# Attention with one shared key head: the order of loads and small steps at the front of the kernel, and the place of token loads and one mask conversion after it

## The chip, the cores and the metric

The kernel runs on one core of a Trainium2 chip. The metric is device time in microseconds (us) of one execution, lower is better. The core has five engines with an instruction queue each: TensorE (PE, matrix products and transposes), VectorE (DVE), ScalarE (ACT), GpSimd (POOL) and SyncE (SP), which here issues nearly all transfers. Each engine takes its instructions strictly in the order in which the program writes them and waits at an instruction until its operands and its buffers are ready; engines wait for each other through semaphores.

## The reference

64 batches of 128 tokens with 512 features. Each is normalised, projected to 16 query heads of 64, and to one key and one value head that all query heads share; a null key and value (from `cond`) stand ahead of the 128 keys. Scores get a bias per head, a mask per batch and a causal mask; the softmax goes over 129 keys. The output projection is normalised again and added to the input.

```python
xn = layernorm(x, g_in)
q = (xn @ Wq).reshape(b, n, H, DH).transpose(0, 2, 1, 3) * scale
kv = xn @ Wkv
k, v = (kv[..., :DH], kv[..., DH:])
k = jnp.concatenate([nk, k], axis=1)      # null key ahead
v = jnp.concatenate([nv, v], axis=1)      # null value ahead
sim = jnp.einsum('bhid,bjd->bhij', q, k) + bias
sim = jnp.where(causal_mask, neg, sim)
sim = jnp.where(mask_p[:, None, None, :], sim, neg)
attn = jax.nn.softmax(sim, axis=-1)
out = jnp.einsum('bhij,bjd->bhid', attn, v)
out = out.transpose(0, 2, 1, 3).reshape(b, n, INNER) @ Wo
x = x + layernorm(out, g_out)
```

All is in float32. The null key and value are subtracted from keys and values, and the null bias from the bias, so that the null column itself is zero before the softmax.

## The kernel before

Four batches make a group, 16 groups in all. For batch `m`, `load_x` brings its tokens (from group 2 on, a mixed quarter of a group's tokens under the same numbering); `norm_stats` (DVE, one small power on POOL), `norm_nmr` (DVE) and `norm_apply` (DVE for group 0, ACT after it) normalise them in place; `norm_T` transposes them on PE with a copy by ACT for groups 0 and 1, `tokens_T` with `tokens_out` and `tokens_in` (DVE and two transfers over DRAM) from group 2 on. `kv_mm` and `kv_out` make keys and values, `keys_T` and `values_spread` bring them into the layout of the products through DRAM. Queries of group 0 come from `q_half(c, h)`, eight chunks `c` for two halves `h` of the group; those of later groups from seven products in place of eight (`product`, with sums of weights and tokens made by `weight_sum` on DVE and `token_sum` on POOL).

Order is written out by hand: instructions go to each engine as the lines of the program stand. It has three parts.

The front (lines 1138 to 1222): group 0 is loaded, normalised and projected, `w_q` and `w_kv` are scaled by the gain (`weights_q`, `weights_kv`), the bias is made causal on POOL (`causal(u)`, u is the half of the heads) and the null bias is taken from it on DVE (`null_shift(u)`), group 1 is normalised. `load_second` issues the loads behind the weights: first half of the bias, null bias, null key and value, second half of the bias, mask of group 0, the null value once more as a column (`nv2`), tokens of batches 4 to 7, mask of group 1. On SP nothing overtakes: a load whose buffer isn't free, or which the queue holds back, holds all behind it. Tokens live in three buffers (`xp`), only batches 3 and 4 in two others; so batch 7 takes the buffer of batch 2 and its load waits for `norm_T(2)`.

The steps (`step_a` for even n, `step_b` for odd n, from n = -2): step n makes a quarter of the queries of a later group and a quarter of its keys and values, the exponentials of batch n+1, and, in `region`, scores of batch n+2 and values of batch n; output products run in pairs of batches. At the end of `step_a` the tokens n+12 and n+13 are loaded, behind the stores of that step. At the end of each fourth `step_b` (f == 3), `mask_neg(g)` turns the mask of the next group into numbers (`mneg`, line 485, DVE); `bias_add` on POOL adds it to the bias, and `scores_add` on DVE (line 528) adds the scores from PSUM.

The last steps (`last_step`) hold no projection and are not touched.

PSUM for scores has one buffer (`ps_s`): the second half of a batch's scores is written only when `scores_add` has read the first. `kv_mm` and `norm_T` share two buffers (`ps_w`).

Of the kernel before, what the change touches and what calls it, by code (L numbers as in the profile page):

```python
# [17 lines left out]
def kernel(  # L18
# [60 lines left out]
    B, N, DIM = x.shape  # L79
# [6 lines left out]
    GB = 4  # L86
    NG = B // GB
# [12 lines left out]
    XB = 3  # L100
# [13 lines left out]
    def load_x(m):  # L114
        g, t = divmod(m, GB)
        pool, tag = (rp, "res") if m in (XB, XB + 1) else (xp, "x")
        xs[m] = pool.tile([P, DIM], FP, tag=tag, name=f"x_{m}")
        if g < 2:
            nc.sync.dma_start(out=xs[m], in_=x[m])
        else:  # L120
            nc.sync.dma_start(
                out=xs[m], in_=x[g * GB : (g + 1) * GB, t * Q : (t + 1) * Q, :]
            )
# [13 lines left out]
    def load_mask(g):  # L137
        m8s[g] = gp.tile([P, TOK], U8, tag="m8", name=f"m8_{g}")
        nc.sync.dma_start(
            out=m8s[g],  # L140
            in_=mask[g * GB : (g + 1) * GB].rearrange("b n -> (b n)").partition_broadcast(P),
        )
# [23 lines left out]
    nc.sync.dma_start(out=wkv, in_=w_kv.rearrange("(kc p) f -> p kc f", p=P))  # L166

    def load_second():
        load_bias(1)
        nc.sync.dma_start(out=nbh, in_=null_bias.partition_broadcast(P))  # L170
        nc.sync.dma_start(
            out=nkv, in_=cond[0:2].rearrange("r d -> (r d)").partition_broadcast(P)
        )
        load_bias(0)
        load_mask(0)
        for r in range(2):
            nc.sync.dma_start(
                out=nv2[r * DH : (r + 1) * DH, :], in_=cond[1].unsqueeze(1)
            )
        for m in range(XB + 1, 2 * GB):  # L180
            load_x(m)
        load_mask(1)

    def load_bias(u):
        rows = slice(u * DH, (u + 1) * DH)
        bias_r = attn_bias.rearrange("(u f r) i j -> u r i f j", u=2, r=2)[u]
        for r in range(2):
            rf = slice(r * NF, (r + 1) * NF)
            nc.sync.dma_start(out=biasp[rows, rf, LK], in_=bias_r[r, 0:DH, :, 0:NL])
            nc.sync.dma_start(out=biasp[rows, rf, UK], in_=bias_r[r, DH:N])  # L190
# [77 lines left out]
    def norm_apply(m):  # L268
        if m >= GB and m not in xnmr:
            norm_nmr(m)  # L270
        mv, rstd = stats.pop(m)
        xm = xs[m]
        if m < GB:
            nc.vector.tensor_scalar(
                xm, xm, mv[:, 0:1], rstd, ALU.subtract, ALU.mult
            )
        else:
            nc.scalar.activation(  # L278
                xm, xm, AF.Identity, bias=xnmr.pop(m), scale=rstd
            )  # L280
# [188 lines left out]
    def q_out(g, c, toks, tag, name=None):  # L469
        lo = toks.start // N  # L470
        o = q_part(g, c, lo, lo + 2)
        p = prod[tag].rearrange("p (t h i) -> p t h i", t=2, h=2)
        if name is None:
            nc.scalar.copy(o, p)  # L474
        else:
            k = kept.pop(name).rearrange("p (t h i) -> p t h i", t=2, h=2)
            nc.vector.tensor_tensor(o, p, k, ALU.add)  # L477
# [302 lines left out]


    def weights_q(kc):
        if kc in (2, 0):
            nc.vector.tensor_scalar(
                wq[:, kc, :], wq[:, kc, :], gin8[:, kc : kc + 1], None, ALU.mult
            )
        else:
            nc.scalar.activation(
                wq[:, kc, :], wq[:, kc, :], AF.Copy, scale=gin8[:, kc : kc + 1]
            )  # L790
# [32 lines left out]
    def step_a(n):  # L823

        g, f = divmod(n + 6, GB)
        q = g < NG
        p12, p4 = n - 1, n - 3
        first, third = paired(p12), paired(p4)
        e, nb = n + 1, n + 2
        soft = 0 < n  # L830
        if q and f == 0 and g + 1 < NG:
            load_mask(g + 1)
        if third:
            out_product(p4, 4, ps_y, "X", start=False)
        if soft:
            exps(e, 0, 0, 3)
        if third:
            pair_stats(p4)
        if n == 2:
            token_sum(g, 3)  # L840
            token_sum(g, 4)
        if 0 < n:
            bias_add(nb)
        if third:
            pair_pow(p4)
            out_part(p4 + 1, 0, "X")
        max_hi()
        kv_late = not first
        if n == 0:
            norm_stats(10)  # L850
            exps(1, 1, 0, 4)
        if q:
            if not kv_late:
                kv_out(n + 6, kv_mm(n + 6))
            if f == 0:
                q_tile(g)
            product(g, f, 1, ps_q, "a")
        if soft:
            exps(e, 0, 3, 6)
        if q:  # L860
            keep("a", "p1")
            product(g, f, 2, ps_w, "w")
            q_out(g, f, lo_t, "w", "p1")
        if soft:
            exps(e, 0, 6)
            rinv(e, 0)
        if q:
            if f == 0 and n > 2:
                token_sum(g, 3)
            product(g, f, 6, ps_q, "a", start=False)  # L870
            keep("a", "u2")
        if n == 0:
            exps(1, 1, 4)
            rinv(1, 1)
            scale(1, 1)
        if soft:
            scale(e, 0)
        if third:
            pair_stats(p4 + 1)
            pair_pow(p4 + 1)  # L880
            pair_nmr(p4)
        if soft:
            exps(e, 1, 0, 2)
        if third:
            pair_norm(p4)
            pair_gain(p4)
            pair_residual(p4)
            store(p4)
        if q:
            if f == 0 and n > 2:  # L890
                token_sum(g, 4)
            product(g, f, 5, ps_q, "c")
        if first:
            out_product(p12, 1, ps_y, "X")
        if soft:
            exps(e, 1, 2, 3)
        if first:
            out_keep("X", "yp1", "yp1")
        if third:
            pair_nmr(p4 + 1)  # L900
        if q:
            product(g, f, 7, ps_q, "a", start=False)
            keep("a", "u3")
            q_out(g, HC + f, hi_t, "c", "u3")
            if kv_late:
                kv_out(n + 6, kv_mm(n + 6))
        if third:
            pair_norm(p4 + 1)
        if first:
            out_product(p12, 2, ps_w, "w")  # L910
        if third:
            pair_gain(p4 + 1)
        if first:
            out_part(p12, 0, "w", "yp1")
        if third:
            pair_residual(p4 + 1)
            store(p4 + 1)
        if q:
            product(g, f, 3, ps_q, "c", start=False)
            q_out(g, f, hi_t, "c", "u2")  # L920
        if soft:
            exps(e, 1, 3)
            rinv(e, 1)
            scale(e, 1)
        if n == 2:
            residual(0)
            store(0)
        if n == -2:
            scores(1, 0)
            scores_add(1, 0)  # L930
            scores_max(1, 0)
            blocks_T(0)
        if n == 0:
            norm_apply(10)
            norm_stats(11)
            tokens_T(10)
            load_x(13)
        if q:
            product(g, f, 4, ps_q, "a", start=False)
            q_out(g, HC + f, lo_t, "a")  # L940
        if n == 0:
            norm_apply(11)
        if n == -2:
            scores(1, 1)
            scores_add(1, 1)
            late_max.append(1)
        for m in (n + 12, n + 13):
            if m < B and n:
                load_x(m)

    def step_b(n):

# [52 lines left out]
        if q:  # L1005
            product(g, f, 7, ps_q, "a", start=False)
            keep("a", "u3")
            q_out(g, HC + f, hi_t, "c", "u3")
            if kv_late:
                kv_out(n + 6, keys_values())  # L1010
            if n == 1:
                out_mm(0)
# [29 lines left out]
        if q:  # L1042
            product(g, f, 4, ps_q, "a", start=False)
            q_out(g, HC + f, lo_t, "a")
            if f == 3:
                keys_T(g)
                values_spread(g)
                if g < NG:
                    mask_neg(g)
        if second:  # L1050
            out_product(p, 3, ps_y, "Y", start=False)
# [102 lines left out]
    norm_stats(3)  # L1154
    q_half(0, 0)
    norm_apply(2)
    norm_T(2)
    q_half(1, 0)
    norm_apply(3)
    norm_T(3)  # L1160
    weights_kv()
    norm_stats(4)
    norm_apply(4)
    q_half(2, 0)
    causal(1)
    norm_stats(5)
    norm_apply(5)
    null_shift(1)
    q_half(3, 0)
    norm_T(4)  # L1170
    for m in range(GB):
        kv_out(m, kv_mm(m))
    norm_stats(6)
    norm_stats(7)
    norm_nmr(6)
# [18 lines left out]
    weight_sum(4)  # L1194
    for c in range(4):
        q_half(c, 1)
    load_late()
    load_x(8)
    load_x(9)
# [75 lines left out]
```

## Time and profile before

| | |
|---|---|
| median of 3 runs | 1103.41 us (1102.82 to 1104.4) |
| the profiled execution's own time | 1104.52 us |
| its span in the profile | 1102.7 us |
| granted TensorE clock, mean | 0.993 |
| PE busy / DVE / ACT / POOL | 1077.4 / 800.9 / 694.9 / 702.1 us |
| from HBM / to HBM | 67.45 MB / 35.65 MB |
| front: PE starts the first scores | 47.88 us |

All times inside the profile are microseconds from the start of the span. PE is TensorE's matmul row, PEld its weight loads, SPq the transfers that SP issues. A row of the timeline has start, duration, engine, line, operation, output and inputs, shapes and count, and in brackets how long the engine had been idle before it and what ended that. Rows merge neighbouring instructions; durations of matmuls overlap a little, so the step from one start to the next is the better measure. The granted clock is given as a share of full speed.

### The profile page before, as it was taken

How to read it: one execution, taken by the hardware profiler on the slowest of the kernel's cores; microseconds unless marked ns; L12 is line 12 of the kernel's file. 1: busy time of each engine (PE TensorE's matmuls, PEld its weight loads, DVE VectorE, ACT ScalarE, POOL GpSimd, SP SyncE). 2: the span in 40 equal slices, each digit the busy share in tenths (PEclk: the TensorE clock that was granted, in tenths of full speed). 3: DMA queues.
4: the chain of work that ended last, by engine and by line, in shares of the span. 5: the costliest groups of instructions: out<-in, count | busy, mean ns of one | idle time of the engine just before them, and what ended most of it. 6: DMA issues, size and time to landing. Idle time of an engine off the chain costs nothing.

```text
span 1102.7 us, 29987 instructions
## 1 busy us (share of the span) xinstructions
PE 1077.4 (98%) x11780; PEld 900.2 (82%) x11780; DVE 800.9 (73%) x1545; ACT 694.9 (63%) x2779; POOL 702.1 (64%) x517
## 2 busy tenths in 40 slices
PE   7999999999999999999999999999999999999997
PEld 6876788888888888888888888888888888888653
DVE  4667578786787878678687787878678787657772
ACT  3355566666766666666666676666676666567682
POOL 2465757676675766757586675767667576665572
PEclk9999999999999999999999999999999999999999
DMA  7414242333334242333324234233333424111211
GB/s 198 139 44 120 77 117 76 112 90 111 82 100 122 70 120 78 118 97 92 105 80 133 69 90 133 70 118 89 112 84 99 121 67 125 58 59 41 68 60 67
DMA packets 67980, 105.03 MB, mean 95 GB/s; under 512 B 8448, under 2 KB 32640, under 8 KB 66048
## 3 DMA queue, kind: packets, MB, share of 16 engines
q1 hardware_dynamic: 67024, 102.07, 31.1%
q8 instruction: 92, 1.51, 0.6%
q10 hardware_dynamic: 816, 1.05, 0.3%
q14 instruction: 48, 0.39, 0.1%
HBM read 67.45 MB, written 35.65 MB: 93 GB/s over the span
## 4 chain that ended last, share of the span: by engine, by line
PE 86%; DVE 7%; ACT 4%; DMA 2%; issue 1%; POOL 0%; SPq 0%; DVEq 0%; ACTq 0%
PE pa L456 17%; PE pyX L689 16%; PE ps L515 9%; PE pc L456 8%; PE pyY L689 7%; PE po L606 7%; PE pkv L327 6%; PE py L636 5%; PE pw L456 5%; PE pyw L689 4%; DVE mneg L485 3%; ACT s L542 3%; PE pq L405 2%; ACT x L278 1%; DVE s L528 1%; DMA x<-in_x_dram 1%
## 5 line engine op out<-in xcount | busy, mean ns | idle before, releaser
L542 ACT ACTIVATE s<-s,nmax 128x65 f32<-128x65 f32 (+1 forms) x1024 | 372.5, 370 | 6.1 <-DVE nmax L533 6.1
L563 POOL TENSOR_TENSOR s<-s,rinv 128x512 f32<-128x512 f32 (+1 forms) x128 | 189.2, 1478 | 184.1 <-DVE rinv L559 177.3
L494 POOL TENSOR_TENSOR s<-biasp,mneg 128x1552 f32<-128x1552 f32 x64 | 206.1, 3220 | 105.4 <-DVE sb L578 103.0
L542 ACT ACTIVATION_READ_ACCUMULATOR s<-s,nmax 128x1 f32 x1024 | 197.6, 193 | 0.0
L622 ACT ACTIVATE oT<-po,nv 128x256 f32<-128x256 f32 x256 | 100.2, 474 | 139.5 <-PE po L606 139.5
L528 DVE TENSOR_TENSOR s<-ps,s 128x512 f32<-128x512 f32 (+1 forms) x128 | 119.9, 936 | 64.9 <-PE ps L515 64.9
L689 PE MATMUL pyX<-wT,oT 128*128 128x256 f32 x672 | 163.2, 386 | 0.0
L689 PEld LDWEIGHTS pyX<-wT,oT 128*128 128x128 f32 x672 | 124.5, 191 | 22.8 <-issue 4.8
L515 PEld LDWEIGHTS ps<-kT,qT 64*64 64x64 f32 x4096 | 90.9, 133 | 40.7 <-issue 29.6
L456 PE MATMUL pa<-xS,wq 128*128 128x256 f32 x480 | 123.5, 380 | 0.0
L533 DVE TENSOR_REDUCE nmax<-s 128x8 f32<-128x520 f32 (+1 forms) x128 | 122.1, 954 | 1.4
L515 PE MATMUL ps<-kT,qT 64*64 64x64 f32 (+1 forms) x4096 | 115.1, 250 | 5.6 <-DVE s L528 4.1
L578 DVE STREAM_TRANSPOSE sb<-s 128x1536 f32<-128x1536 f32 x64 | 113.5, 1773 | 8.0 <-POOL s L563 3.8
L456 PEld LDWEIGHTS pa<-xS,wq 128*128 128x128 f32 x480 | 91.4, 191 | 12.6
L606 PE MATMUL po<-sb,vr 32*64 32x128 f32 (+1 forms) x3584 | 99.7, 322 | 0.3 <-ACT qT L474 0.3
L606 PEld LDWEIGHTS po<-sb,vr 32*64 32x64 f32 x3584 | 79.4, 131 | 10.9 <-DVE y L760 0.8
L467 ACT COPY ku<-pa 128x256 f32<-128x256 f32 x120 | 44.7, 372 | 65.4 <-PE pa L456 64.1
L477 DVE TENSOR_TENSOR qT<-pc,ku 128x256 f32<-128x256 f32 x120 | 49.7, 414 | 42.6 <-ACT ku L467 35.3
L327 PE MATMUL pkv<-wkv,xT 128*128 128x128 f32 x512 | 73.6, 290 | 1.0 <-ACT xT L290 1.0
L327 PEld LDWEIGHTS pkv<-wkv,xT 128*128 128x128 f32 x512 | 67.3, 199 | 8.0 <-issue 5.2
L278 ACT ACTIVATE x<-x,nmr,rstd 128x512 f32<-128x512 f32 x60 | 48.5, 814 | 32.6 <-DVE nmr L265 31.7
L456 PE MATMUL pc<-xT,wS 128*128 128x256 f32 x240 | 62.0, 381 | 3.6 <-DVE qT L477 3.5
(95 smaller groups left out, 1926.7 us busy)
## 6 DMA issues: line engine op xcount, KB each, us to landing
x<-in_x_dram SPq DMA_DIRECT2D x64, 256.0 KB
res<-in_x_dram SPq DMA_DIRECT2D x64, 256.0 KB
out_dram<-y SPq DMA_DIRECT2D x64, 256.0 KB
xd<-xb SPq DMA_DIRECT2D x14, 1024.0 KB
xT<-xd SPq DMA_DIRECT2D x56, 256.0 KB
vr<-vd SPq DMA_DIRECT2D x64, 128.0 KB
kT<-kd SPq DMA_DIRECT2D x64, 64.0 KB
kd<-kb SPq DMA_DIRECT2D x16, 128.0 KB
```

The costliest lines, as they stand in the source:

```text
L327: nc.tensor.matmul(pkv, xT[g][:, t, kc, :], wkv[:, kc, :], start=(kc == 0), stop=(kc == KC - 1),)
L456: nc.tensor.matmul(prod[tag], w[:, kc, f * P : (f + 1) * P], t[:, :, kc, :], start=(start and kc == 0), stop=(kc == HK - 1), skip_group_ch ...
L494: nc.gpsimd.tensor_tensor(S[b], biasp, mneg[:, t].unsqueeze(1).broadcast_to([P, R8, ROW]), ALU.add,)
L515: nc.tensor.matmul(pv[u * DH : (u + 1) * DH, r, f, :], qT[g][rows, f, t, hf, u], kT[g][rows, 0 : nk // Q, t, :], start=True, stop=True,)
L528: nc.vector.tensor_tensor(sv, pss.pop((b, hf)), sv, ALU.add)
L533: nc.vector.tensor_reduce(nmax[b][:, hf], S[b][:, :, WITH_NULL[hf]], AX.X, ALU.max, negate=True)
L542: nc.scalar.activation(row, row, AF.Exp, bias=nmax[b][:, hf, k : k + 1], accum_out=rsum[b][:, hf, k : k + 1],)
L563: nc.gpsimd.tensor_tensor(sv, sv, rinvs.pop((b, hf)).unsqueeze(2).broadcast_to([P, R8, sv.shape[2]]), ALU.mult,)
L578: nc.vector.transpose(sb.rearrange("p j e q -> p e j q"), S[b][:, :, 1 : ROW - 1].rearrange("p e (j k) -> p e j k", k=Q),)
L606: nc.tensor.matmul(po[s][rows] if both else po[s][rows, 1:2], vr[g][quad, j, t, :], sb[quad, slots, r * NF : (r + 1) * NF, :], start=(j == 0),
L622: nc.scalar.activation(oT[b][:, u * NF : (u + 1) * NF, :].rearrange("p f (h i q) -> p i h f q", h=2, i=2)[:, i], po, AF.Identity, bias=nv2,)
L689: nc.tensor.matmul(prod[key], h[:, c, :], w[:, c, :], start=(start and c == 0), stop=(c == HC - 1), skip_group_check=not start,)
```

## The change

The loads at the front are put into another order: tokens of batch 4 come before the first half of the bias, those of batches 5 to 7 before the second half, and the null value column (`nv2`) goes behind the second half of group 0's queries. VectorE scales three chunks of `w_q` (0, 2, 3), not two. Normalisation of batch 3 comes before `q_half(1, 0)`, `norm_T(2)` and `norm_T(3)` come one `q_half` later each, and the null bias of the first half (`null_shift(1)`) goes behind the keys and values of group 0. In the even steps the token loads go from the end to the beginning. The mask conversion of group 1 goes, in step 1, ahead of the last parts of that step; for later groups it stays.

```diff
     def load_second():
+        load_x(XB + 1)
         load_bias(1)
         nc.sync.dma_start(out=nbh, in_=null_bias.partition_broadcast(P))
         nc.sync.dma_start(
             out=nkv, in_=cond[0:2].rearrange("r d -> (r d)").partition_broadcast(P)
         )
+        for m in range(XB + 2, 2 * GB):
+            load_x(m)
         load_bias(0)
         load_mask(0)
+        load_mask(1)
+
+    def load_null_value():
         for r in range(2):
             nc.sync.dma_start(
                 out=nv2[r * DH : (r + 1) * DH, :], in_=cond[1].unsqueeze(1)
             )
-        for m in range(XB + 1, 2 * GB):
-            load_x(m)
-        load_mask(1)
...
     def weights_q(kc):
-        if kc in (2, 0):
+        if kc != 1:
...
         soft = 0 < n
+        for m in (n + 12, n + 13):
+            if m < B and n:
+                load_x(m)
         if q and f == 0 and g + 1 < NG:
             load_mask(g + 1)
...
             late_max.append(1)
-        for m in (n + 12, n + 13):
-            if m < B and n:
-                load_x(m)
...
             q_out(g, HC + f, hi_t, "c", "u3")
+            if n == 1:
+                mask_neg(g)
             if kv_late:
                 kv_out(n + 6, keys_values())
...
                 values_spread(g)
-                if g < NG:
+                if n > 1:
                     mask_neg(g)
...
     norm_apply(2)
+    norm_apply(3)
+    q_half(1, 0)
     norm_T(2)
-    q_half(1, 0)
-    norm_apply(3)
-    norm_T(3)
     weights_kv()
     norm_stats(4)
     norm_apply(4)
     q_half(2, 0)
+    norm_T(3)
     causal(1)
     norm_stats(5)
     norm_apply(5)
-    null_shift(1)
     q_half(3, 0)
     norm_T(4)
     for m in range(GB):
         kv_out(m, kv_mm(m))
+    null_shift(1)
     norm_stats(6)
...
         q_half(c, 1)
+    load_null_value()
     load_late()
```

## The prediction

> **What bounds the kernel now.** The first part of the page gives the busy time of each engine:
>
> ```profile
> span 1102.7 us, 29987 instructions
> PE 1077.4 (98%) x11780; PEld 900.2 (82%) x11780; DVE 800.9 (73%) x1545; ACT 694.9 (63%) x2779; POOL 702.1 (64%) x517
> ```
>
> TensorE is the bound, with 25 us not busy. A change of loads and order can win these, and whatever the clock loses after them; so the second view is the list of TensorE's waits in the first 150 us (cause; total, times, longest):
>
> ```profile
> PE pxT L289 <- ACT x L278: 4.5, 1, 4.5
> PE pc L456 <- DVE qT L477: 3.5, 3, 2.3
> PE ps L515 <- DVE s L528: 2.5, 1, 2.5
> ...
> PE pkv L327 <- ACT xT L290: 1.0, 1, 1.0
> ```
>
> The same list for 150 to 1000 us is empty. The third view, the granted clock by windows (columns: stretch, its length, busy PE, PEld, DVE, ACT, POOL; clock; DMA share; GB/s), shows what a wait costs beyond itself:
>
> ```profile
> 25.40:32.10 6.70, 5.72 (x27) 5.42 (x27) 3.01 (x6) 1.55 (x3) 0.49 (x1) 0.50 0.00 0
> 107.30:110.60 3.30, 3.30 (x12) 2.85 (x11) 3.23 (x6) 1.65 (x10) 0.30 (x1) 0.50 0.44 124
> 134.60:137.90 3.30, 3.30 (x9) 2.67 (x8) 1.69 (x5) 1.96 (x9) 3.24 (x2) 0.50 0.37 156
> 138.00:1000.00 862.00, 860.50 (x9727) 740.00 (x9726) 654.18 (x1279) 568.14 (x2281) 571.51 (x415) 1.00 0.33 96
> ```
>
> Each of the three long waits is followed by a stretch at half clock; after 138 us TensorE is always busy at full clock. So what TensorE gains by 138 us stays gained, unless a new wait appears later. The fourth view is the timeline around the waits (start, duration, what, idle before and its cause):
>
> ```profile
> 24.62 0.66 PE L289 MATMUL pxT<-ident,x 128*128 128x128 f32 x4 [4.50 <-ACT x L278]
> 27.78 5.03 PE L327 MATMUL pkv<-wkv,xT 128*128 128x128 f32 x24 [0.98 <-ACT xT L290]
> 105.74 1.10 PE L515 MATMUL ps<-kT,qT 64*64 64x128 f32 x32 [2.45 <-DVE s L528]
> 133.40 1.13 PE L456 MATMUL pc<-xT,wS 128*128 128x256 f32 x4 [2.29 <-DVE qT L477]
> ...
> 21.67 0.69 DVE L252 BATCH_NORM_STATS2 st<-x 128x6 f32<-128x512 f32 x1 [7.06 <-DMA x<-in_x_dram]
> 39.16 0.61 DVE L485 TENSOR_SCALAR mneg<-m 128x256 f32<-128x256 uint8 x2
> 101.71 3.38 DVE L485 TENSOR_SCALAR mneg<-m 128x256 f32<-128x256 uint8 x2
> 129.36 0.69 DVE L252 BATCH_NORM_STATS2 st<-x 128x6 f32<-128x512 f32 x1 [2.06 <-DMA x<-in_x_dram]
> 131.91 0.69 DVE L252 BATCH_NORM_STATS2 st<-x 128x6 f32<-128x512 f32 x1 [1.45 <-DMA x<-in_x_dram]
> ...
> 18.79 2.01 SPq L119 DMA_DIRECT2D x<-in_x_dram  x4
> 122.50 1.16 SPq L121 DMA_DIRECT2D x<-in_x_dram  x2
> ```
>
> Behind the first wait stand the tokens of batch 4, issued at 18.79 and used at 21.67; behind the second the mask conversion, 3.38 us in front of a score addition; behind the third tokens 14 and 15, issued at 122.50 behind the store of batch 0, which the queue held 11.5 us for POOL.
>
> **The front, step by step.** All times are of the profiled execution.
>
> *Scaling w_q.* Chunk 3 goes from ScalarE (2.41 us for two, 1.2 each) to VectorE (1.41 for two, 0.7). Its data were there when ScalarE began at 10.90, so VectorE does it 10.9 to 11.6 and statistics of batches 2 and 3 start 1.1 us later (11.5, not 10.46). Chunk 1 still lands at 12.14 and keeps ScalarE to 13.3, so TensorE's last wait for weights still ends at 13.36: worth 0. The delayed tokens 2 and 3 are ready at 14.1 and 15.0; q_half(1,0), now before norm_T(2), covers that until 15.8.
>
> *Batch 4.* Its issue takes the place of the first bias part, 6.92. It lands between 9.8 (the 2.9 us from issue to use at 18.79) and 14.4 (w_kv, just ahead of it, is what SP waits for until 13.74; 0.7 us more to pass). VectorE reaches its statistics only at 15.55 (x2, x3 normalised, w_kv scaled 0.68), so both ends cost nothing. From statistics to ScalarE's normalisation is 2.1 us (21.67 to 23.75): 17.6 to 18.4. TensorE by then: q(1,0) to 15.8, T(2) 16.2, q(2,0) 17.95, T(3) 18.4, q(3,0) 20.1 (1.73 a half, 0.44 a transpose). No wait; the 4.50 are gone.
>
> *Batch 5* is next in line. Its issue follows nkv and two held issues, about 13.74; landing between 16.6 (2.9 later) and 19.5 (the DMA share falls to 0.09 in 18 to 20, so all issued by 16.3 had landed). I take 17.9, nearer the former plus x4's share of the line. On POOL causal(1), 1.71, stands before its power, so normalisation runs 20.1 to 20.9, q(3,0)'s copy and T(4)'s follow (0.35, 0.6): the second kv product starts at 21.7 after a gap of 0.3. Landing at 19.5 would make that gap 1.7 wider.
>
> *kv products.* Four at full clock take 0.87 each: done at 24.3, against 32.65 before; 8.4 won here.
>
> *The null bias behind the keys* costs VectorE 0.17 + 1.75, now between the fourth kvt and the statistics of batch 6: these begin at 26.45. ScalarE's normalisation of batch 6 ends 3.05 us after that start (33.06 to 36.12 before): 29.5. TensorE is through q(4,0), T(5), q(5,0) at 28.15 and so waits 1.4 for T(6). This is what is late next. Gain then 7.0: scores(0,0) start at 40.85, not 47.88.
>
> *Cover of the rest.* Load 7 is held by norm_T(2) until 16.2, and bias(0) (four issues of 0.6) and both masks queue behind it; causal(0) wants that bias at 29.2, and 19.2 plus the 5 us in which all of it drained before is 24.2. Weight sums shift with the mask (7.2 us) and end at 40.8, scores_add(0,0) wants VectorE at 41.5. The null value (2 issues, 2.39) now delays w_o: its issue is at 38.6 and had 9.2 us to land before (DMA share down at 52), so 47.8; POOL wants it at 55.9, values_out(0) the null value near 79. Nothing.
>
> **The mask of group 1.** It moves to 94.5, where VectorE idles 3.56 us before 100.35 and TensorE runs out_mm(0) for 6.87. Price between 0.61 (39.16, POOL idle) and 3.38 (101.71, POOL busy); POOL idles from 94.85 to 101.62, so I take 0.61. Even 3.38 ends at 97.9; nmr and ScalarE's two passes (1.51) follow, and the transpose (0.7) ends at 100.3, before qT. Queued behind it are only those. The score addition starts at 101.85 and the wait of 2.45 goes. With it goes the half clock: pkv, pa and pw, start to start, took 1.44, 1.71, 1.25 against 0.99, 0.87, 0.86 a step later, 1.68 more. Sum 4.1. Next late: POOL's second token sum, ready at 106.2, wanted at 107.
>
> **Token loads at the head of step_a.** At n=2 tokens 14 and 15 are issued after the values of group 1 (110.1), not 122.50. The second landed 9.4 us after the issue row (131.91); even so both are there at 119.5, VectorE wants them at 127.3. VectorE gains 3.5, TensorE the 2.29 wait and the half clock after it (pyX 3.18 for 1.73, pa 1.09 for 0.86: 1.68). Sum 4.0. Mask 3 and the stores behind the loads find the slots free: those tokens were transposed one step earlier. In the 24 later even steps the same move can win nothing, since TensorE never waits there; what it can cost is bounded by the last rival below. I take 0: no wait of SP for a token slot is listed after 150 us, and the issues fall into SP's own idle time (178.5 us of waiting for the store's operands).
>
> **A rule against this.** The rows: a wait of 2.45 and one of 2.29 each brought 3.3 us or more at 0.50. The Trainium skill, TensorE: Matmul & The Clock Gate, section HAM oscillation, gives as its rule "no PE-idle gaps >~3.4µs". By it the two shorter waits should have cost only themselves and the sum would be 3.4 smaller; the trace disagrees, and I go by the trace.
>
> **Sum.** 7.0 + 4.1 + 4.0 = 15.1. The profiled execution took 1104.52 (span 1102.7 and 1.8 around it), so 1089.4; the median of the runs, 1103.41, lies 1.1 lower: 1088.3.
>
> **Rivals.**
> - The front gives back more: batch 5 late (1.7) and the new wait before T(6), then over 2.2 us, brings half clock (1.7). Gain 11.7: 1091.7. For it: a wait of 2.29 brought the half clock. Against it: the wait of 1.11 that ends at 73.46 did not (the clock was 1.00 from 32.2 to 103.8), and 1.4 lies nearer to that.
> - One of the two later waits stays, because another operand is late (POOL's token sum has 0.8 of room), or because tokens 14's slow landing belongs to this execution alone: 4 less, 1092.3.
> - No change: the front's gain is eaten before 138 by w_o or a later load, and the rest stays within 0.2% (2.2 us): some 1103. It needs w_o 9 us later than worked out.
> - Slower: the loads at the head of each step_a block SP until a slot is free, stores and y buffers come late and TensorE waits in every pair of steps. 15.1 over 24 steps: from 0.63 us a step it eats all, from 0.72 the kernel is slower; at 1.0, 24 − 15.1 gives 1112. Against it: the slots are free one step earlier, and the stores themselves wait 11 us at the longest without TensorE waiting.
>
> **How the numbers follow.** Forecast 0.62, front rival 0.14, one wait stays 0.14, no change 0.04, slower 0.06. A measurement tells about 0.2%. Faster 0.90, same 0.04, slower 0.06. The range holds the first three: below, 1085.5, with batch 6's gap of 1.4 not there and the waits of 0.7 and 0.5 before pa (59.35, 75.91) gone besides; above, 1095, with the first two rivals' losses nearly together (7.4 of 15.1 lost gives 1095.7).
>
> **What would show it.** In the changed profile: no 4.5 wait before pxT, first scores near 41, no half clock before them; a wait of about 1.4 for batch 6's x; mneg of group 1 near 87.5 taking 0.6; pc of group 2 without wait; from 138 − 15 on the same rows as now. A half-clock window around 30, or waits in the even steps after 150, would make me wrong.

## The result, and the profile after

The changed kernel takes 1089.72 us in the median of four runs (1089.33 to 1091.42), the kernel before 1103.91 on the same chip: a ratio of 0.9875, 95% interval 0.9858 to 0.9892, 14.2 us by the medians. The forecast was 1088.3 with a range of 1085.5 to 1095. The profiled execution took 1091.42 and has a span of 1089.1; the three others have spans of 1087.4, 1087.6 and 1087.6. Line numbers are some 3 to 5 higher than before: the kv products are L330, the queries of group 0 L408, the mask conversion L488.

The list of TensorE's waits in the first 150 us, after the change (cause; total, times, longest):

```profile
PE pxT L292 <- ACT x L281: 1.6, 1, 1.6
PE busy L1140 <- POOL nhalf L230: 1.4, 1, 1.4
PE pq L408 <- ACT wq L791: 1.1, 1, 1.1
PE pc L459 <- DVE qT L480: 1.1, 1, 1.1
PE pa L459 <- ACT kp L470: 0.7, 1, 0.7
```

The waits of 4.5, 2.45 and 2.29 us are gone. The one long newcomer stands first in the list: 1.6 us for the normalised tokens of batch 6, the wait that the forecast had put at 1.4.

The first scores before, for comparison:

```profile
47.88 0.69 PE L515 MATMUL ps<-kT,qT 64*64 64x64 f32 x32
```

The timeline of the changed kernel at the three places, with the rows of VectorE and SP behind them (start, duration, engine, line, operation, tiles, count, idle before):

```profile
20.41 4.10 PE L330 MATMUL pkv<-wkv,xT 128*128 128x128 f32 x32
29.99 0.66 PE L292 MATMUL pxT<-ident,x 128*128 128x128 f32 x4 [1.58 <-ACT x L281]
41.38 0.69 PE L518 MATMUL ps<-kT,qT 64*64 64x64 f32 x32
96.72 1.10 PE L518 MATMUL ps<-kT,qT 64*64 64x128 f32 x32
120.27 1.03 PE L459 MATMUL pc<-xT,wS 128*128 128x256 f32 x4
...
15.47 0.69 DVE L255 BATCH_NORM_STATS2 st<-x 128x6 f32<-128x512 f32 x1
25.07 1.76 DVE L216 TENSOR_TENSOR biasp<-biasp,nbp 64x1536 f32<-64x1536 f32 x1
26.86 0.69 DVE L255 BATCH_NORM_STATS2 st<-x 128x6 f32<-128x512 f32 x1
87.95 0.62 DVE L488 TENSOR_SCALAR mneg<-m 128x256 f32<-128x256 uint8 x2
116.54 0.64 DVE L255 BATCH_NORM_STATS2 st<-x 128x6 f32<-128x512 f32 x1
...
6.83 0.33 SPq L119 DMA_DIRECT2D x<-in_x_dram  x1
103.60 1.21 SPq L121 DMA_DIRECT2D x<-in_x_dram  x2
```

Tokens 4 are issued at 6.83 and their statistics no longer wait (15.47, no bracket). The four kv products run from 20.41 to 24.35 without a listed wait and the first scores start at 41.38, against 47.88 before. The conversion of the mask takes 0.62 us at 87.95, not 3.38 in front of the score addition, so the second half of batch 3's scores (96.72) follows without a wait. Tokens 14 are issued at 103.60 and used at 116.54 without a wait, and pc at 120.27 has none.

The granted clock of the same execution, by windows (stretch, length, busy PE, PEld, DVE, ACT, POOL; clock; DMA share; GB/s):

```profile
25.40:32.10 6.70, 5.12 (x28) 4.23 (x28) 5.29 (x12) 3.12 (x6) 2.76 (x4) 1.00 0.06 20
96.30:99.60 3.30, 3.30 (x68) 2.87 (x56) 3.03 (x3) 3.12 (x15) 3.22 (x3) 1.00 0.24 73
138.00:1000.00 862.00, 860.50 (x9729) 740.19 (x9728) 654.02 (x1280) 570.74 (x2292) 573.13 (x417) 1.00 0.31 95
1000.00:1053.10 53.10, 51.02 (x680) 32.14 (x682) 36.28 (x64) 37.96 (x173) 35.21 (x23) 1.00 0.18 56
1053.20:1056.50 3.30, 3.30 (x34) 2.12 (x31) 2.58 (x3) 3.30 (x18) 2.42 (x2) 0.50 0.01 3
```

No stretch at half clock is left up to 1053 us; one has come at 1053. It follows a wait of 1.62 us at the end that both kernels have and that brought nothing in the profiled execution of before. The first row is of the kernel before, the second of the changed one:

```profile
1068.14 1.10 PE L515 MATMUL ps<-kT,qT 64*64 64x128 f32 x32 [1.61 <-DVE s L528]
1053.03 1.87 PE L518 MATMUL ps<-kT,qT 64*64 64x128 f32 x32 [1.62 <-DVE s L531]
```

Where the time went is read by laying the same instruction of both profiles side by side:

| instruction | before | after | difference | step |
|---|---|---|---|---|
| first scores of batch 0 | 47.88 | 41.38 | −6.50 | front −6.5 |
| pa of group 2, product 6 | 111.17 | 100.48 | −10.69 | mask −4.2 |
| pyY of pair 1, product 3 | 138.64 | 123.73 | −14.91 | token loads −4.2 |
| ps at the end of the paired steps | 1007.29 | 992.18 | −15.11 | −0.2 in 870 us |
| last 24 products py | 1086.27 | 1072.80 | −13.47 | given back +1.6 |

The 1.6 given back look like this execution's own: its half-clock stretch near the end makes the rows from 1053.03 to 1062.76 take 9.73 us where before took 8.10, and its span is 1.5 to 1.7 longer than those of the three others.

### The profile page after: what moved, and what is told of

It is laid out like the page before. It is cut to its first block, busy times and chain, and to the rows that moved or that the text cites. A ratio compares the mean times of both kernels' runs of the same rounds, so it can differ in the third digit from the quotient of the medians.

```text
span 1089.1 us, 30001 instructions
## 1 busy us (share of the span) xinstructions
PE 1072.7 (98%) x11780; PEld 896.2 (82%) x11780; DVE 797.4 (73%) x1546; ACT 693.6 (64%) x2778; POOL 702.3 (64%) x517
## 4 chain that ended last, share of the span: by engine, by line
PE 86%; DVE 7%; ACT 4%; issue 1%; DMA 1%; POOL 0%; SPq 0%; DVEq 0%; POOLq 0%; ACTq 0%
PE pa L459 18%; PE pyX L692 16%; PE ps L518 9%; PE pc L459 8%; PE pyY L692 7%; PE po L609 7%; PE pkv L330 6%; PE py L639 5%; PE pw L459 5%; PE pyw L692 4%; DVE mneg L488 3%; ACT s L545 2%; PE pq L408 1%; ACT x L281 1%; DVE s L531 1%
## 5 line engine op out<-in xcount | busy, mean ns | idle before, releaser
L330 PE MATMUL pkv<-wkv,xT 128*128 128x128 f32 x512 | 70.4, 281 | 0.1
L330 PEld LDWEIGHTS pkv<-wkv,xT 128*128 128x128 f32 x512 | 64.3, 191 | 7.0 <-issue 5.0
L749 DVE TENSOR_TENSOR yn<-yn,gob 128x512 f32<-128x512 f32 x56 | 39.2, 700 | 36.1 <-ACT yn L746 36.1
L281 ACT ACTIVATE x<-x,nmr,rstd 128x512 f32<-128x512 f32 x60 | 48.6, 814 | 25.8 <-DVE nmr L268 24.3
## 6 DMA issues: line engine op xcount, KB each, us to landing
vr<-vd SPq DMA_DIRECT2D x64, 128.0 KB, 2.7
kd<-kb SPq DMA_DIRECT2D x16, 128.0 KB, 1.7
```

Source lines behind the costliest of these rows:

```text
L330: nc.tensor.matmul(pkv, xT[g][:, t, kc, :], wkv[:, kc, :], start=(kc == 0), stop=(kc == KC - 1),)
```

## The experiments

Theory: three gains that add up, each a wait of TensorE and the half clock after it. Rivals: that a part only shifts its wait, that the later two depend on the first, that the instruction order at the front matters as much as the loads, and that the half clock has another cause than the idle time. Each time is a median, "faster" is the difference of medians, and behind each ratio stands its 95% interval; ratios are against the kernel before on the same chip and in the same job, whose medians were 1104.33 (first four kernels), 1104.00 (the next four) and 1104.63 (the last two).

### One part alone: token loads at the head of step_a

```diff
--- before
         e, nb = n + 1, n + 2
         soft = 0 < n
+        for m in (n + 12, n + 13):
+            if m < B and n:
+                load_x(m)
...
             late_max.append(1)
-        for m in (n + 12, n + 13):
-            if m < B and n:
-                load_x(m)
 
     def step_b(n):
```

> The kernel before with one part of the change alone: the token loads at the head of step_a. Theory (tokens 14 and 15 are issued too late, behind a store, and the wait they cause also brings a half-clock stretch): 2.3 of wait and 1.7 of slow rows go, 4.0 us faster, about 1099.5, with no wait of TensorE near 133 and the waits near 20 and 105 unchanged. Rival 1 (the slow landing of these tokens belonged to one execution): 0, about 1103.5. Rival 2 (loads ahead of stores hold the stores up in every pair of steps): slower, with waits of TensorE after 150 us.

1100.10 us, ratio 0.9960 (0.9942 to 0.9977): 4.2 faster. The profile has the mask's wait with its half clock, and none near 130:

```profile
103.94 1.58 PE L515 MATMUL ps<-kT,qT 64*64 64x128 f32 x32 [2.45 <-DVE s L528]
105.45 2.07 PE L327 MATMUL pkv<-wkv,xT 128*128 128x128 f32 x8
129.07 1.03 PE L456 MATMUL pc<-xT,wS 128*128 128x256 f32 x4
```

The wait for tokens 14 and 15 was no accident of one execution: the profiles of the four kernels below that keep these loads in their old place (the mask alone, the front alone, the front's loads alone, TensorE kept busy) all hold it, with 2.29 to 2.96 us. From 106 to 1000 us TensorE waits for nothing here: loads ahead of the stores hold it up nowhere. Rival 2, the forecast's own rival for a slower kernel, is out.

### One part alone: the mask conversion of group 1

```diff
--- before
             q_out(g, HC + f, hi_t, "c", "u3")
+            if n == 1:
+                mask_neg(g)
...
-                if g < NG:
+                if n > 1:
                     mask_neg(g)
```

> The kernel before with only the mask conversion of group 1 moved forward. Theory (3.38 us of VectorE in front of the score addition cause 2.45 us of wait and 1.7 us of half-clock rows): 4.1 us faster, about 1099.4; the conversion takes 0.6 in its new place, where POOL idles. Rival 1 (a wait of 2.45 us costs only itself): 2.4 faster, about 1101.1. Rival 2 (the score addition is held by something else, or the conversion delays the normalisation of tokens 12 and 13): 0 to 1 us.

1099.62 us, ratio 0.9959 (0.9941 to 0.9977): 4.7 faster by the medians. The interval, 2.5 to 6.5 us, hardly leaves room for the 2.4 of rival 1; the stages set side by side below (4.2) leave none. The rows show both halves: here the scores (101.24) follow at full clock, while the wait for tokens 15 stays, with slow rows after it (pyX 3.32, not 1.89).

```profile
101.24 1.10 PE L515 MATMUL ps<-kT,qT 64*64 64x128 f32 x32
102.27 1.16 PE L327 MATMUL pkv<-wkv,xT 128*128 128x128 f32 x8
127.28 1.43 PE L456 MATMUL pc<-xT,wS 128*128 128x256 f32 x4 [2.32 <-DVE qT L477]
128.50 3.32 PE L689 MATMUL pyX<-wT,oT 128*128 128x256 f32 x8
92.47 0.62 DVE L485 TENSOR_SCALAR mneg<-m 128x256 f32<-128x256 uint8 x2
```

### One part alone: the front

The diff takes the two parts above back out of the changed kernel.

```diff
--- after
         soft = 0 < n
-        for m in (n + 12, n + 13):
-            if m < B and n:
-                load_x(m)
...
             late_max.append(1)
+        for m in (n + 12, n + 13):
+            if m < B and n:
+                load_x(m)
...
             q_out(g, HC + f, hi_t, "c", "u3")
-            if n == 1:
-                mask_neg(g)
...
-                if n > 1:
+                if g < NG:
                     mask_neg(g)
```

> The whole front of the change, without the move of the token loads in the steps and of the mask conversion. Theory (the three gains stand by themselves): first scores 6.5 us earlier, time about 1097, and the waits of 2.4 us near 99 and 2.3 near 127 are still there, each with its half-clock stretch where the phase falls so. Rival (the front's gain is partly given back, because the late tokens 14 and 15 depend on times that don't move): 3 to 5 us only, and a longer wait near 127.

1098.13 us, ratio 0.9938 (0.9918 to 0.9959): 6.2 faster. First scores start at 41.52. TensorE's waits in the whole run still hold both later ones, each followed by a half-clock stretch (100.7 to 104.0 and 128.0 to 131.3 at 0.50). The first row adds the 2.45 near 99 and the 1.6 at the end:

```profile
PE ps L518 <- DVE s L531: 4.1, 2, 2.4
PE pc L459 <- DVE qT L480: 3.6, 3, 2.3
PE pxT L292 <- ACT x L281: 1.6, 1, 1.6
```

The parts add up: 4.2 + 4.7 + 6.2 = 15.1, against 14.2 for the whole, though each median is uncertain by some 2 us either way. The profiles are sharper when the same instructions are set side by side within each of them: the start of the first scores, the step from there to product 6 of group 2 (`pa`, the second row of the table above), and from there to product 3 of pair 1 (`pyY`, the third row).

| profile | first scores | to product 6 | to product 3 of pair 1 |
|---|---|---|---|
| before | 47.88 | 63.29 | 27.47 |
| token loads alone | 46.06 | 63.24 | 23.23 |
| mask alone | 45.89 | 59.11 | 27.53 |
| front alone | 41.52 | 63.30 | 27.47 |
| all three | 41.38 | 59.10 | 23.25 |

The mask takes 4.2 us out of the second column and neither of the others does; the token loads take 4.2 out of the third. So these two gains depend neither on each other nor on the front. The first column shows something else: the first three kernels have the same front, and their first scores start up to 2.0 us apart from one execution to the next (44.56 in the kernel with TensorE kept busy, below). What the front is worth therefore depends on the execution it is compared with.

### The front's loads without its instruction order

```diff
--- before
     def load_second():
+        load_x(XB + 1)
         load_bias(1)
...
+        for m in range(XB + 2, 2 * GB):
+            load_x(m)
         load_bias(0)
         load_mask(0)
+        load_mask(1)
+
+    def load_null_value():
         for r in range(2):
...
-        for m in range(XB + 1, 2 * GB):
-            load_x(m)
-        load_mask(1)
...
         q_half(c, 1)
+    load_null_value()
     load_late()
```

> Only the order of the loads at the front is changed (tokens of 4 first, 5 to 7 before the second half of the bias, null value late); the order of the instructions on TensorE, VectorE and ScalarE is that of before. Theory (the 4.5 us wait was the tokens' late landing and nothing else): the front gains at least as much as with the order of instructions, 6.5 us or more, since the null bias then stands before the keys and batch 6 is normalised without the wait of 1.6; 6.5 to 8 us, about 1095.5 to 1097. Rival (the instruction order is needed too, since VectorE takes the null bias and the statistics of 5 before the keys): 2 to 4 us, about 1100.

1096.03 us, ratio 0.9920 (0.9893 to 0.9946): 8.3 faster, more than the whole front; its four runs (1094.72 to 1097.31) all lie under the four of the front alone (1097.87 to 1098.32). First scores start at 39.40, 2.1 earlier than with the new instruction order, and TensorE waits for no tokens at the front:

```profile
26.33 1.89 PE L408 MATMUL pq<-xT,wq 128*128 128x256 f32 x8
28.06 0.60 PE L292 MATMUL pxT<-ident,x 128*128 128x128 f32 x4
39.40 0.69 PE L518 MATMUL ps<-kT,qT 64*64 64x64 f32 x32
24.58 0.68 DVE L255 BATCH_NORM_STATS2 st<-x 128x6 f32<-128x512 f32 x1
```

Here VectorE takes the null bias off at 19.63, while TensorE still projects, and batch 6's statistics start at 24.58, 2.3 before those of the changed kernel. So the whole gain of the front is the loads', and the reordered instructions cost about 2 us of it. (The new instruction order without the moved loads was not run.)

### The yardstick, the null bias further back, and the loads with everything old

The changed kernel again on the chip of the next experiments:

> The changed kernel once more, as the yardstick for the next two on the same chip. Theory (its 15.1 us of gain hold; a half-clock stretch in the last 40 us, worth 1.6, comes in some executions and not in others): 13.5 to 15.2 us under the kernel before.

1089.82 us, ratio 0.9879 (0.9858 to 0.9899): 14.2 under the kernel before, as expected. Three of its four executions have spans from 1087.5 to 1088.0, one has 1089.9; in the profiled one (1088.0) the wait of 1.6 near the end is there, and the clock is 1.00 from 1000 to 1085. So the wait near the end comes without the stretch too.

```diff
--- after: the null bias of half 1 behind the normalisation of batches 6 and 7
         kv_out(m, kv_mm(m))
-    null_shift(1)
...
     values_spread(0)
+    null_shift(1)
     null_shift(0)
```

> The changed kernel with the null bias of the first half taken off directly before that of the second half, that is behind the normalisation of batches 6 and 7. Theory (the new wait of 1.6 us ahead of batch 6's transpose is the null bias standing in front of its statistics): that wait goes, first scores near 39.8 and 1.6 us faster than the changed kernel. Rival (the weight sums and the mask behind it come later and hold the first score addition): the wait moves to the first scores, 0 to 0.5 us.

1088.95 us, ratio 0.9865 (0.9847 to 0.9883); by medians 0.9 under the yardstick. The intervals overlap, but all four runs (1088.18 to 1089.10) lie under all four of the yardstick (1089.32 to 1092.22). The profile is sharper: the transpose of batch 6 runs at 28.56 without a wait and the first scores start at 39.89, 1.9 before those of the yardstick's profile (41.80) and 1.5 before those of the first profile of the changed kernel.

```profile
28.56 0.60 PE L292 MATMUL pxT<-ident,x 128*128 128x128 f32 x4
39.89 0.69 PE L518 MATMUL ps<-kT,qT 64*64 64x64 f32 x32
```

VectorE pays with 2.60 us for that null bias, now beside POOL's causal(0), where it took 1.76 in the changed kernel; the first score addition comes right behind the weight sums, at 41.04, and TensorE doesn't wait for it. The theory holds at the place: the wait is the null bias. In the whole time the direction shows, the size does not.

```diff
--- after: w_q, transposes 2 and 3 and the null bias as in the kernel before
-        if kc != 1:
+        if kc in (2, 0):
...
     norm_apply(2)
+    norm_T(2)
+    q_half(1, 0)
     norm_apply(3)
-    q_half(1, 0)
-    norm_T(2)
+    norm_T(3)
...
     q_half(2, 0)
-    norm_T(3)
     causal(1)
     norm_stats(5)
     norm_apply(5)
+    null_shift(1)
     q_half(3, 0)
...
         kv_out(m, kv_mm(m))
-    null_shift(1)
     norm_stats(6)
```

> All moves of loads and of the mask conversion, but none of the other instructions at the front: third chunk of w_q on ScalarE, transposes 2 and 3 and the null bias where they stood before. Theory (the front's gain is the loads' alone, and the new order of instructions costs 2 us of it): first scores at 39.4, not 41.4, no wait of 1.6 ahead of batch 6, and 2.0 us faster than the changed kernel, some 17 us under the kernel before. Rival (the 2 us saved at the front are taken back by the mask, the key round trip or the second token sum near 97): as fast as the changed kernel.

1087.40 us (1087.08 to 1088.00), ratio 0.9853 (0.9835 to 0.9871): 16.6 under the kernel before and 2.4 under the yardstick of the same chip, whose fastest run (1089.32) is slower than its slowest. First scores start at 39.00, 2.8 before those of the yardstick's profile. The rival, that the 2 us are taken back later, is out.

```profile
39.00 0.69 PE L518 MATMUL ps<-kT,qT 64*64 64x64 f32 x32
```

### Two chunks of w_q on VectorE, all else as changed

```diff
--- after
-        if kc != 1:
+        if kc in (2, 0):
```

> The changed kernel with chunk 3 of w_q scaled by ScalarE as before (two chunks each). Theory (the last wait for weights is set by the landing of chunk 1 and ScalarE's 1.2 us after it, so the change of engine is worth 0): the wait for weights ends within 0.3 us of 13.4, first scores at 41.4, time as the changed kernel within 0.5 us. Rival (ScalarE is late with chunk 1 when it has chunk 3 ahead of it): 0.5 to 1.2 us slower than the changed kernel.

1090.18 us, ratio 0.9879 (0.9852 to 0.9906), 14.5 under the kernel before of its job, much as the changed kernel in its two jobs (14.2 and 14.2). At the place the last wait for weights ends at 14.03, not within 0.3 of 13.4; in the profiles that hold the change's own order it ends at 13.38 to 13.73. The first scores start at 41.77, within the 41.38 to 41.80 of those profiles. ScalarE begins only at 11.54, when its first chunk has landed, and its two passes of 1.2 follow one another. In the profile of before that start was 10.90, so part of the 0.65 between 13.38 and 14.03 is the landing of this execution; how much is the engine's was not separated.

### TensorE kept busy in the wait

The kernel before computes on; eleven products of the identity are added, whose result is not used.

```diff
--- before
+        if n == 1:
+            pb = ps_y.tile([P, P], FP, tag="Y", name="busy_in_wait")
+            for _ in range(11):
+                nc.tensor.matmul(pb, ident, ident, start=True, stop=True)
         if nb < B:
             scores(nb, 1)
```

> The kernel before with eleven products of the identity, whose result nobody reads, on TensorE between the values of batch 1 and the second half of the scores of batch 3, where it waits 2.45 us for VectorE. The wait for VectorE stays, but TensorE isn't idle in it. Theory (idle time of this length is what brings the half clock): the stretch at 0.50 near 107 goes, 1.7 us faster. Rival (the half clock there has another cause, or its rows are slow for VectorE's sake): no faster, and the stretch stays.

1100.99 us, ratio 0.9978 (0.9964 to 0.9993): 0.8 to 4.0 us faster although work was added. The added products fill the wait and all behind them runs at full clock (the kernel before needed 1.64 and 1.91 for pkv and pa):

```profile
99.90 2.72 PE L817 MATMUL busy_in_wait<-ident 128*128 128x128 f32 x22
102.55 1.10 PE L515 MATMUL ps<-kT,qT 64*64 64x128 f32 x32
103.58 1.16 PE L327 MATMUL pkv<-wkv,xT 128*128 128x128 f32 x8
104.58 1.03 PE L456 MATMUL pa<-xT,wq 128*128 128x256 f32 x4
```

VectorE is as late as before (these scores start 57.99 us behind the first ones, against 57.86). From the first scores to product 6 the kernel takes 61.75 us, 1.5 less than before; the 3.0 between the medians are more than that, with an interval wide enough for both. So what slows the rows is TensorE's idle time, and a wait of 2.45 us is enough. In the same run the wait for tokens 15, 2.96 here, keeps its stretch at 0.50 (128.9 to 132.2).

### The wait at the end

To the best version so far, the second half of batch 60's output product is moved ahead of batch 63's first scores.

```diff
--- e9_loads_only_all
-        if n == B - 2:
-            out_mm(n - 2, HC)
...
-        out_mm(n - 1, 0, NC if n < B - 3 else HC)
+        out_mm(n - 1, 0, NC if n < B - 2 else HC)
```

> All moves of loads and of the mask, the front's instructions as before, and besides the second half of batch 60's output product ahead of the first scores of batch 63, not behind its region. Theory (the wait of 1.6 us near the end is VectorE, held by the exponentials' sums of batch 62, and 3.5 us more work for TensorE ahead of it cover it): that wait goes, and with it the half-clock stretch that some executions have in the last 40 us; 1.6 to 3 us faster than all moves alone, about 18 to 20 us under the kernel before. Rival (the last values then wait for the exponentials of batch 63): the wait moves there, 0.

1085.47 us (1085.33 to 1086.12), ratio 0.9840 (0.9807 to 0.9872): 19.2 under the kernel before, 1.9 under all moves alone by medians from two jobs. Inside the profiles the last stretch, from the last `pyw` to the last output products, takes 80.84 us; it is 82.53 in all nine others that have no half clock there, so 1.7 are won at this place. This beats both kernels. The wait near 1053 is gone and none has come behind it:

```profile
1043.54 7.13 PE L639 MATMUL py<-wo,oT 128*128 128x512 f32 x16
1050.60 0.69 PE L518 MATMUL ps<-kT,qT 64*64 64x64 f32 x32
1051.23 1.56 PE L609 MATMUL po<-sb,vr 32*64 32x256 f32 x56
1052.71 1.10 PE L518 MATMUL ps<-kT,qT 64*64 64x128 f32 x32
```

## Why the prediction was right

By its own steps:

- *Scaling w_q, worth 0.* Right: the last wait for weights ends at 13.38 (13.36 before), and undoing this part gave the same time.
- *Batch 4.* Statistics at 15.47 (forecast 15.55), normalised from 17.54 (17.6). *Batch 5:* normalised from 19.95 (20.1), held by causal(1) on POOL and not by its landing. *kv products* done at 24.35 (24.3).
- *Null bias, and the new wait of 1.4.* The mechanism was right, the size 0.2 short: the fourth kvt starts at 24.55 and the null bias runs to 26.83, so batch 6's statistics come at 26.86, not 26.45; 26.45 less 0.17 and 1.75 is 24.53, the start of that kvt, whose own 0.29 the forecast left out. The front gave 6.5 in these two profiles, not 7.0. Both figures stand on one execution of the kernel before, with its first scores at 47.88; the same front had them at 46.06, 45.89 and 44.56 in the three other profiles that keep it, and the changed front at 41.38 to 41.80. Pair by pair the front is worth 2.8 to 6.5. Whether the execution behind the forecast was a usual one was not asked; it was (1104.52, with medians of 1103.4 to 1104.6), and to that extent the size at the front is luck. What the forecast didn't ask was whether the instruction order is needed at all; the runs showed that the loads alone give 8.3.
- *Mask.* 0.62 us in the new place, for which 0.61 was taken, the row where POOL idles. Gain 4.2 for 4.1. The Trainium skill (SBUF — State Buffer, section SBUF: two separate sides) states that VectorE and GpSimd share a port pair, and that of a GpSimd instruction and a VectorE instruction in a two-port mode the one that starts first has the pair for its whole duration while the other blocks. The row of 0.62 and the one of 3.38 beside a busy POOL fit this; whether the conversion runs in such a mode no run here shows.
- *Token loads.* 4.2 for 4.0; nothing in the 24 later steps, as taken.
- *Sum.* 15.1 was forecast; the two profiles differ by 15.1 at the last paired step. Missed was the end: the wait of 1.6 there, left out as unchanged, brought a half-clock stretch, worth 1.6 us, in the profiled execution; the one yardstick run with a span of 1089.9 and a lower mean clock (0.998, the others 0.999 to 1.000) looks like another case. In the executions without it the kernel stands at 1089.3 to 1090.0. That is still 1.0 to 1.7 over 1088.3, while the spans of the three in the first job, 1087.4 to 1087.6, are 15.1 to 15.3 under the span of before (1087.5 to 1088.0 in the yardstick's job): the forecast took the median of the first three runs as 1.1 below the profiled execution, and that offset didn't carry over.

The rule weighed in the prediction, no idle time of TensorE beyond 3.4 us (the Trainium skill, TensorE: Matmul & The Clock Gate, section HAM oscillation), put the sum at 11.7. Waits of 2.3 to 3.0 us were followed by a stretch at 0.50 in each profile that holds one, and filling one of them removed its stretch. The measurement decides against the rule as a limit for this kernel. The wait of 1.1 had none after it, nor had the new one of 1.58 at the front (1.00 from 25.4 to 32.1); the one of 1.62 at the end has it in some executions. On what the difference hangs was not tried.

## What to carry to other kernels

Where one engine is busy for 98% and its few waits stand at the start, list them with the clock of the next 4 us: here three waits of 9.2 us together were worth 15. Look for what the late operand stood behind on its queue, a load behind a store or a conversion in front of an addition, and move that alone first: the loads by themselves won 8.3 us at the front, and the instructions reordered around them took 2 back. What a piece of work costs can change with its place: the mask conversion took 0.6 us where POOL was idle and 3.4 beside a busy POOL. And take more than one profile of the kernel before: in four profiles that hold its front unchanged, the first scores start up to 3.3 us apart.

## What the runs showed that was not expected

The same wait of 1.6 us near the end costs 1.6 or 3.2 us from one execution to the next, by the clock alone: eleven profiles hold it, and two of them (the changed kernel's first and that of the mask alone) have a half-clock stretch behind it.

A half-clock stretch doesn't start where the wait ends. In the profile of before the three waits end at 24.62, 105.74 and 133.40, and the clock falls at 25.36, 107.28 and 134.59; these falls lie 24 times and 8 times 3.41 us apart, and the stretches last 6.83, 3.41 and 3.41 us. But where a wait lies between two such points does not decide alone: the 1.62 near the end lies wholly between two of them in the changed kernel (1051.41 to 1053.03, the clock falls at 1053.20) and also in the front alone (1060.07 to 1061.69, between 1059.83 and 1063.24 by the steps counted back from its fall at 1093.96), where it brought none.

The wait at the front, unchanged in four of the kernels, was 4.5, 3.9, 3.6 and 3.5 us in their profiles. It follows the time at which SP issues the tokens of batch 4 (18.79, 17.92, 17.89 and 17.55): their statistics start 2.9 us after the issue in all four. So it is the issue, behind the loads ahead of it on the queue, that varies, and not the landing after it.

The runs of the kernel before spread from 1100.4 to 1106.6 in one job, while those of the version with all loads moved stayed within 1087.1 and 1088.0.
